# Top-1 expert layer behind a cross-attention: the second gathered tile turned later, the second scatter of each expert sooner, and the last four tiles finished without an accumulating transfer

## The chip, the core and the metric

The kernel runs on one core of a Trainium2 chip. The core has five engines with a queue of instructions each: TensorE (PE in the profile, with its weight loads as PEld), VectorE (DVE), ScalarE (ACT), GpSimd (POOL) and SyncE (SP). An engine takes its instructions in the order in which the program lists them, and waits on semaphores for the others. SP, ACT and POOL also issue DMA transfers. The metric is the device time of one execution in microseconds (us), and less is better. All data are float32.

## What is computed

Two layers act on 16 sequences of 128 tokens with 256 features each, 2048 tokens in all. The first is a cross-attention with 16 heads. The second, where all of the change lies, is a feed-forward layer with eight experts and a shared expert. Every token goes to the one expert that scores highest, and every token also goes through the shared expert:

```python
scores_aE = x_aD @ router_DE
vals_aK, idx_aK = jax.lax.top_k(scores_aE, K)                      # K = 1
masked_aE = jnp.full_like(scores_aE, -jnp.inf).at[jnp.arange(a)[:, None], idx_aK].set(vals_aK)
gates_Ea = jax.nn.sigmoid(masked_aE).T
routed_in_EaD = gates_Ea[:, :, None] * x_aD[None, :, :]
mid_EaF = silu(einsum('ead,edf->eaf', routed_in_EaD, w1_eDF)) * einsum('ead,edf->eaf', routed_in_EaD, w3_eDF)
routed_out_EaD = einsum('eaf,efd->ead', mid_EaF, w2_eFD)
shared_aD = silu(x_aD @ ws1_DF) * (x_aD @ ws3_DF) @ ws2_FD
out_aD = shared_aD + routed_out_EaD.sum(axis=0)
x = x + out_aD.reshape(b, s, d)
```

Here D is 256 and the hidden size F is 704. In the kernel `x` ahead of this layer is written to `out` first, and everything later is added to it in HBM.

## The kernel before

The attention takes the first 470 us of the span, and none of the change lies there. Then a part of the shared expert runs while the router sorts the tokens, and from about 555 us on the eight experts run one after the other. The kernel sorts the experts by their number of tokens. The expert in position w has a window of `WINDOWS[w]` slots (320, then three of 288, then four of 256). The first 256 slots make two tiles of 128 tokens, 2w and 2w+1. The slots beyond 256 of the first four experts are gathered into two further tiles, called the rest tiles, 16 and 17.

**One expert.** Its hidden values are made in five units of 128 hidden features (`expert_unit`), each of seven matrix products that PE, ACT, DVE and POOL share, and a last piece of 64 features (`expert_rest`). POOL's part of a unit is two operations, lines 2036 and 2037.

**How tokens come in.** For each tile POOL issues an indirect DMA that gathers 128 rows from the table `h_rows` in HBM (`gather`, line 1737). `turn_tile` then lets DVE multiply the rows with the gates (line 1748) and transpose them in blocks of 32 (line 1777), and SP stores the result in HBM (`x_blocks`, line 1778). `fetch_inputs` lets SP read it back as the transposed input `xT` (line 1785). DVE makes sums of it for the next expert (`token_ops`, lines 1900 to 1903).

**How results go out.** The second product of an expert makes rows of the output (`out_pieces`, line 1854, into the banks `rD`), ACT copies them to SBUF (`sg`, line 1863) and POOL issues an indirect DMA that adds them to the rows of `out` (`scatter`, line 1866). Each such scatter waits for the one before it, because rows of any token may come from any tile.

**What sets the order.** The program writes it out. Each step is handed to `plan` with a time, and at the end all steps are sorted by these times and issued in that order. One expert has 35 places; `base` is 35 (w - 1), and one place is about 0.42 us in this part of the trace. So a changed time changes nothing but the order of the instructions in each engine's queue. While an expert w runs, `expert_asides(w)` plans the second products and the scatters of expert w - 1, and the gathers, turns and fetches for expert w + 2.

**The end.** The shared expert's hidden values for the last four tiles of 128 tokens (rows 12 to 15 of `out`, seen as 16 tiles) are held in SBUF. After the last expert, `held` makes their second product (PE line 218, into the banks `yh`). For the first two, ACT copies the result to SBUF (line 427) and POOL adds it to `out` with one accumulating transfer of 256 KB (line 431). For the last two, SP and ACT read the rows of `out` back (line 429), DVE adds (line 437), and SP and ACT store them (line 438). The read and the accumulation wait for the last scatter.

The steps that the change touches are these lines of `expert_asides`:

```python
plan(base + 22 + (28 if w < E - 1 else 14) * i, down[(NF + 1) * i + NF])   # scatter of tile i
plan(base - 5 + 5 * i, lambda i=i: gather(2 * w + 4 + i))
plan(base + 19.2 + 7 * i, lambda i=i: turn_tile(2 * w + 4 + i))
```

Of the kernel before, what the change touches and what calls it, by code (L numbers as in the profile page):

```python
# [9 lines left out]
F32 = mybir.dt.float32  # L10
I32 = mybir.dt.int32
AF = mybir.ActivationFunctionType
ALU = mybir.AluOpType
# [4 lines left out]
P = 128  # L18
# [9 lines left out]
def resampler_attn__then__top1_moe_kernel(  # L28
# [17 lines left out]
    nc = tc.nc  # L46
    B, S, D = x.shape
    INNER = wq_t.shape[1]
    E, F = w1.shape[0], w1.shape[2]
# [14 lines left out]
    NF = FC + 1  # L64
# [13 lines left out]
    mwork = ctx.enter_context(tc.tile_pool(name="mwork", bufs=2, side="right"))  # L78
# [63 lines left out]
    shared, scattered = {}, []  # L142
    x_stored, added = {}, []

    def behind(dma, others, reason):
        for o in others:
            tc.add_manual_dep(
                dma.ins,
                o.ins.name,
                mybir.DependencyInfo(mybir.DependencyClass.Sync, mybir.DependencyReason.DATA),  # L150
                reason=reason,
            )
        return dma
# [62 lines left out]
    def down_half(t, mid, i, py, order=range(FC + 1)):  # L216
        for n, f in enumerate(order):
            nc.tensor.matmul(
                py,
                lhsT=mid[:, f, ts(i, P)],  # L220
                rhs=shared["wd"][:, f, :],
                start=(n == 0),
                stop=(n == FC),
            )
            yield n
# [185 lines left out]
    def held():  # L411

        reason = "rows of any token may come from any tile"
        ways = [nc.sync, nc.scalar]
        sent, back = [
            mwork.tile([P, 2, D], F32, tag="xr", name=f"held_{k}", bufs=3) for k in range(2)
        ]
        pys = []
        for n in range(4):
            py = early_half[0][0]  # L420
            if n:
                py = ps_t.tile([P, D], F32, tag="T", name=f"yh_{n}")
                for _ in down_half(n, shared["held"][:, n // 2], n % 2, py):
                    pass
            pys.append(py)
            if n < 2:
                nc.scalar.copy(sent[:, n, :], py)
        for n in (2, 3):
            load = ways[n % 2].dma_start(out=back[:, n - 2, :], in_=out[B - 4 + n])
            behind(load, scattered, reason)  # L430
        add = nc.gpsimd.dma_start(
            out=out[B - 4 : B - 2].rearrange("b p d -> p b d"), in_=sent, accum_op=ALU.add
        )
        behind(add, scattered, reason)
        for n in (2, 3):
            xr = back[:, n - 2, :]
            nc.vector.tensor_tensor(xr, pys[n], xr, ALU.add)
            ways[n % 2].dma_start(out=out[B - 4 + n], in_=xr)

    consts = {}  # L440

# [59 lines left out]
    with ExitStack() as at:  # L501
# [35 lines left out]
        def load_keys(k):  # L537
# [11 lines left out]
            out=wv, in_=wkv_t[:, INNER : 2 * INNER].rearrange("(c p) e -> p c e", p=P)  # L549
# [1179 lines left out]
    for w in range(NREST):  # L1729
        at = sum(REST[:w])  # L1730
# [4 lines left out]
    def gather(t, tag="xg"):  # L1735
        xg = rwork.tile([P, D], F32, tag=tag, name=f"xg_{t}")
        nc.gpsimd.indirect_dma_start(
            out=xg,
            out_offset=None,
            in_=h_rows,  # L1740
            in_offset=Offset(ap=routing["table"][:, t : t + 1], axis=0),
            bounds_check=NT,
            oob_is_err=False,
        )
        xgs[t] = xg

    def gate(t):
        nc.vector.tensor_scalar(xgs[t], xgs[t], routing["gates"][:, t : t + 1], None, ALU.mult)
# [24 lines left out]
    def turn_tile(t):  # L1773

        gate(t)
        px = rwork.tile([P, DC, NB, BL], F32, tag="xp", name=f"xp_{t}")
        nc.vector.transpose(px, xgs.pop(t).rearrange("p (c k j) -> p c j k", c=DC, k=BL))
        nc.sync.dma_start(
            out=x_blocks[:, ts(t % 2, NB)].rearrange("c i k j q -> (i k) c (j q)"),
            in_=px.rearrange("p c j q -> p c (j q)"),  # L1780
        )

    def fetch_inputs(w):
        for c in range(DC):
            nc.sync.dma_start(
                out=inputs_t[w % NREST][:, c, 0 : 2 * P].rearrange("p (i q) -> p i q", q=BL),
                in_=x_blocks[c].rearrange("i k j q -> (k j) i q"),
            )

    def expert_of(w, engine):  # L1790
        return engine.value_load(routing["expert"][0:1, w : w + 1], min_val=0, max_val=E - 1)

    def load_up(k, w, engine=nc.sync):
        e = expert_of(w, engine)
        a1, a3 = (a[ds(e, 1)].rearrange("e (c p) f -> p (e c) f", p=P) for a in (w1, w3))
        engine.dma_start(out=w13s[k][:, :, 0:F], in_=a1)
        engine.dma_start(out=w13s[k][:, :, F : F + FR], in_=a3[:, :, FC * P : F])
        engine.dma_start(out=w13s[k][:, :, F + FR : 2 * F], in_=a3[:, :, 0 : FC * P])

    def load_down(k, w, engine=nc.sync):  # L1800
        e = expert_of(w, engine)
        a2 = w2[ds(e, 1)]
        engine.dma_start(
            out=w2s[k][:, 0:FC, :],
            in_=a2[:, 0 : FC * P, :].rearrange("e (c p) d -> p (e c) d", p=P),
        )
        engine.dma_start(
            out=w2s[k][:, FC, :], in_=a2[:, F - P : F, :].rearrange("e p d -> p (e d)")
        )
# [96 lines left out]
    def weight_ops(w):  # L1906

        s = sums_of[w % 2]
        w13 = w13s[w % 3]
        lo, hi = (w13[:, :, ds(at, FC * P)] for at in (0, F + FR))  # L1910
        op = nc.vector.tensor_tensor
        return [
            lambda: op(s[:, 0], hi[:, 0], hi[:, 1], ALU.add),
            lambda: op(s[:, 1], s[:, 0], lo[:, 0], ALU.subtract),
            lambda: op(s[:, 2], lo[:, 1], s[:, 1], ALU.subtract),
            lambda: op(hi[:, 0], lo[:, 0], hi[:, 0], ALU.subtract),
        ]
# [31 lines left out]
    def window_pieces(w):  # L1949
        return [  # L1950
            f
            for i in range(2)
            for f in out_pieces(
                2 * w + i,
                [(slice(0, P), mids[w % 5][:, :, ts(i, P)], w2s[w % 5])],
                last_but,
            )
        ]
# [5 lines left out]
    def rest_pieces(k):  # L1964
        parts = [(slice(at, at + BL), mids[w][:, :, ds(to, BL)], w2s[w]) for w, at, to in rests[k]]
        return out_pieces(2 * E + k, parts)
# [16 lines left out]
    def plan(time, f):  # L1983
        schedule.append((time, len(schedule), f))
# [110 lines left out]
    def expert_asides(w):  # L2095

        base = 35 * (w - 1)
        down = window_pieces(w - 1) if w else []

        if 1 <= w < E - 2:  # L2100
            plan(base + 10.6, lambda: load_up((w + 2) % 3, w + 2))
        if w + 2 < E:
            plan(base + 32, lambda: fetch_inputs(w + 2))
        for i in range(2):
            for k in range(NF):
                if w:
                    plan(base + 0.7 + 2.8 * (NF * i + k), down[(NF + 1) * i + k])
                else:
                    plan(base + 0.7 + 2.5 * (NF * i + k), last_down)
            if w:  # L2110
                plan(base + 22 + (28 if w < E - 1 else 14) * i, down[(NF + 1) * i + NF])
            if w + 2 < E:
                plan(base - 5 + 5 * i, lambda i=i: gather(2 * w + 4 + i))
                plan(base + 19.2 + 7 * i, lambda i=i: turn_tile(2 * w + 4 + i))
        if w in rest_at:
            for k, f in enumerate(rest_pieces(rest_at[w])):
                plan(base + (33.6 if k < NF else 44.5), f)
        if NREST <= w < E - 1:
            plan(base + 33.8, lambda: load_down((w + 1) % 5, w + 1))
        if w + 1 < E:  # L2120
            for k, o in enumerate(weight_ops(w + 1)):
                plan(base + (10.2, 12.2, 23.8, 33.9)[k], o)
            for k, o in enumerate(token_ops(w + 1)):
                plan(base + (16.6, 16.7, 30.6, 30.7)[k], o)

    number = 0
    for w in range(E):
        for f in range(FC):
            expert_unit(w, f, number)
            number += 1  # L2130
        expert_rest(w)
        expert_asides(w)
# [8 lines left out]
    end = 35 * (E - 2)  # L2141
    down = window_pieces(E - 1)
    for i, times in (
        (1, (33.9, 34.9, 35.9, 36.5, 37.2, 39.6, 40.5)),
        (0, (37.6, 38.5, 39.1, 42.0, 42.4, 45.5, 46.0)),
    ):
        for k, at in enumerate(times):
            plan(end + at, down[(NF + 1) * i + k])
# [6 lines left out]
    def ending():  # L2155
        held()
# [131 lines left out]
```

## Time and profile before

| | |
|---|---|
| runs | 698.91, 700.80 and 701.86 us, median 700.80 |
| the profiled execution | 700.42 us, of which the span from the first to the last instruction is 698.7 us |
| granted TensorE clock | 0.998 |
| PE busy | 686.4 us, 98% of the span |
| DVE, ACT, POOL busy | 465.3, 361.1 and 358.2 us |
| PE in the experts' part | idle for 1.0 us in all (one wait, at line 1854) |
| POOL at line 1866 | 9 waits for the scatter before, 15.7 us in all |

The profile is that of one execution. In a line of the timeline the columns are the start in us, the duration, the engine, the line and operation, out<-in with shapes, how many, and in brackets the idle time of that engine just before with what ended it. In the chain of waits a line gives a start, a length and what the time was spent on; it is followed back from the last instruction.

### The profile page before, as it was taken

What the parts mean: (1) busy time and instruction counts of PE and PEld (TensorE: products, weight loads), DVE (VectorE), ACT (ScalarE), POOL (GpSimd) and SP (SyncE); (2) the same over time, 40 slices, a digit from 0 to 9 for tenths busy, and PEclk for the clock granted to TensorE, in tenths of its full rate; (3) what the DMA queues carried; (4) which work ended last, traced back from release to release, by engine and by line L of the source; (5) the groups of instructions that cost most, each with busy time, mean ns of one, the idle gap of its engine ahead of it and who ended that gap; (6) DMA issues with size and microseconds to landing.
All of it is one profiled execution on the core that took longest, in us unless ns stands there. A gap on an engine that the chain in (4) does not pass through costs nothing.

```text
span 698.7 us, 12751 instructions
## 1 busy us (share of the span) xinstructions
PE 686.4 (98%) x4390; PEld 585.5 (84%) x4390; DVE 465.3 (67%) x1033; ACT 361.1 (52%) x1085; POOL 358.2 (51%) x546
## 2 busy tenths in 40 slices
PE   9999999999999999999999999999999999999996
PEld 6778888888888888888888887887788899988895
DVE  7658677778678688678758657647826467756530
ACT  3556466456555655655655555514336455545440
POOL 4258536535545446436435433513466477767662
PEclk9999999999999999999999999999999999999999
DMA  7275855865766685685684594533492156767523
GB/s 247 92 227 188 225 179 182 222 202 193 202 209 202 191 241 175 213 219 176 205 220 166 164 295 166 186 87 46 166 337 63 22 134 170 158 144 203 121 28 64
DMA packets 142042, 121.07 MB, mean 173 GB/s; under 512 B 61329, under 2 KB 128146, under 8 KB 141970
## 3 DMA queue, kind: packets, MB, share of 16 engines
q1 hardware_dynamic: 135602, 111.20, 52.5%
q0 software_dynamic: 5792, 8.46, 6.9%
q8 instruction: 37, 0.61, 0.4%
q10 hardware_dynamic: 576, 0.52, 0.2%
q14 instruction: 35, 0.29, 0.1%
HBM read 71.40 MB, written 48.92 MB: 172 GB/s over the span
## 4 chain that ended last, share of the span: by engine, by line
PE 85%; DMA 6%; DVE 3%; ACT 2%; issue 1%; POOL 1%; POOLq 0%; DVEq 0%; ACTq 0%; SPq 0%
PE O L968 9%; PE S L903 8%; PE pw L987 8%; PE pq L730 8%; PE skX L849 5%; PE svX L849 5%; PE rD L1854 5%; PE rX L2020 4%; PE skZ L849 3%; PE skY L849 3%; PE svY L849 3%; PE svZ L849 3%; PE rYZ L2020 3%; PE pX L293 3%; DMA out_dram<-sg,table 3%; PE p L191 2%
## 5 line engine op out<-in xcount | busy, mean ns | idle before, releaser
L935 POOL TENSOR_SCALAR pe<-pe,rs 128x256 f32<-128x256 f32 x256 | 130.3, 527 | 217.0 <-DVE rs L932 216.9
L922 ACT ACTIVATE pe<-S,nmx 128x256 f32<-128x256 f32 x256 | 119.0, 483 | 54.8 <-DVE nmx L915 54.8
L915 DVE TENSOR_REDUCE nmx<-S 128x4 f32<-128x1024 f32 x64 | 75.4, 1220 | 27.5 <-PE S L903 27.5
L944 DVE STREAM_TRANSPOSE px<-pe 128x512 f32<-128x512 f32 x128 | 82.4, 683 | 0.2
L987 PE MATMUL pw<-wo,oT 128*128 128x256 f32 x256 | 66.2, 385 | 0.0
L730 PE MATMUL pq<-kvT,early 128*128 128x256 f32 x256 | 65.9, 385 | 0.0
L968 PEld LDWEIGHTS O<-pT,v 128*64 128x64 f32 x1024 | 55.2, 137 | 12.2 <-issue 5.6
L968 PE MATMUL O<-pT,v 128*64 128x128 f32 x1024 | 63.2, 276 | 1.3 <-DMA pT<-p_blocks 1.2
L903 PE MATMUL S<-kT,qT 64*128 64x256 f32 x512 | 63.9, 389 | 0.0
L979 ACT COPY oT<-O 128x512 f32<-128x512 f32 x32 | 18.7, 586 | 86.5 <-PE O L968 86.5
L1854 PE MATMUL rD<-w,mid_w 128*128 128x256 f32 (+1 forms) x252 | 61.8, 380 | 1.0 <-ACT sg L1863 1.0
L730 PEld LDWEIGHTS pq<-kvT,early 128*128 128x128 f32 x256 | 47.5, 190 | 10.9 <-issue 5.1
L987 PEld LDWEIGHTS pw<-wo,oT 128*128 128x128 f32 x256 | 47.5, 190 | 10.5 <-issue 4.6
L903 PEld LDWEIGHTS S<-kT,qT 64*128 64x128 f32 x512 | 46.8, 186 | 10.5 <-issue 6.2
L922 ACT ACTIVATION_READ_ACCUMULATOR pe<-S,nmx 128x1 f32 x256 | 54.6, 213 | 0.0
L932 DVE RECIPROCAL rs<-sums 128x4 f32<-128x4 f32 x64 | 11.3, 177 | 56.3 <-ACT pe L922 56.1
L1866 POOL DMA_INDIRECT out_dram<-sg,table x18 | 29.5, 1637 | 19.8 <-DMA out_dram<-sg,table 15.7
L1854 PEld LDWEIGHTS rD<-w,mid_w 128*128 128x128 f32 (+1 forms) x252 | 32.9, 172 | 4.1 <-ACT sg L1863 1.4
L2036 POOL TENSOR_TENSOR mid_w<-mid_w,hT 128x128 f32<-128x128 f32 (+2 forms) x40 | 29.3, 733 | 11.6 <-ACT mid_w L2035 11.4
L868 ACT COPY v<-svX 128x512 f32<-128x512 f32 x45 | 26.6, 592 | 12.0 <-PE svX L849 11.6
L849 PE MATMUL svY<-wv,kvT 128*128 128x256 f32 x120 | 30.9, 380 | 0.4 <-DVE v L873 0.4
L849 PE MATMUL svX<-wv,kvT 128*128 128x256 f32 x120 | 31.1, 382 | 0.0
(365 smaller groups left out, 1538.7 us busy)
## 6 DMA issues: line engine op xcount, KB each, us to landing
p_blocks<-px SPq DMA_DIRECT2D x64, 512.0 KB, 2.9
pT<-p_blocks SPq DMA_DIRECT2D x64, 512.0 KB, 4.3
w<-in_w_dram SPq DMA_DIRECT2D x16, 640.0 KB, 7.4
w<-in_w_dram SPq DMA_DIRECT2D x8, 704.0 KB, 5.9
t_blocks<-tx SPq DMA_DIRECT2D x12, 256.0 KB, 2.3
kvT<-t_blocks SPq DMA_DIRECT2D x12, 256.0 KB, 6.4
out_dram<-xres SPq DMA_DIRECT2D x8, 256.0 KB, 4.8
h_rows<-h SPq DMA_DIRECT2D x8, 256.0 KB, 4.2
```

The source lines that it names most:

```text
L730: nc.tensor.matmul(pqs[g, j][:, jj], lhsT=wq[:, c, ts(2 * j + jj, P)], rhs=kvTs[g][:, c, :, 1, :], start=(c == 0), stop=(c == DC - 1),)
L849: nc.tensor.matmul(o[:, a, :], lhsT=left, rhs=right, start=(first and a == 0), stop=(a == 1), skip_group_check=True,)
L903: nc.tensor.matmul(pl[:, r, j, :], lhsT=qTs[g, h][rows, k, i, :], rhs=kTs[g, h][rows, i, k, :], start=True, stop=True,)
L915: nc.vector.tensor_reduce(nmx, pl, AX.X, ALU.max, negate=True)
L922: nc.scalar.activation(pes[u][:, h, :], pl[:, r, j, :], AF.Exp, bias=nmx[:, r, j : j + 1], accum_out=sums[u][:, h : h + 1],)
L935: nc.gpsimd.tensor_scalar(w, w, rs[:, i : i + 1], 1.0, ALU.mult, ALU.mult)
L944: nc.vector.transpose(px[:, :, t].rearrange("p j h q -> p h j q"), pes[u][:, ts(n, 4), ts(t, S)].rearrange("p h (j k) -> p h j k", k=BL),)
L968: nc.tensor.matmul(o[r * HD : (r + 1) * HD, j, :], lhsT=vs[g, h][:, i, t, ts(2 * j + r, HD)], rhs=pTs[u][:, j // 2, :, t, 2 * (j % 2) + r, :],
L987: nc.tensor.matmul(pws[b], lhsT=outT[u][:, k % HC, :], rhs=wo[:, k, :], start=(k == 0), stop=(k == NP - 1))
L1854: nc.tensor.matmul(py[0][rows, :], lhsT=mid[:, f, :], rhs=wd[:, f, :], start=(k == 0), stop=(k == NF - 1),)
L1866: add = nc.gpsimd.indirect_dma_start(out=out_rows, out_offset=Offset(ap=routing["table"][0:n, t : t + 1], axis=0), in_=py[1][0:n, :], in_o ...
L2020: nc.tensor.matmul({2: Y, 3: Z, 5: Z}.get(n, X), lhsT=lhsT, rhs=rhs, start=n in (1, 2), stop=True, skip_group_check=True,)
```

## The change

It has three parts.

1. In the plan, the second of the two turns of an expert moves from place 26.2 to 31.2, and the first from 19.2 to 20.2; the fetch moves from 32 to 37 and the load of the second weights from 33.8 to 37.2. The second scatter of an expert moves from place 50 to 38, and the last step of a rest tile from 44.5 to 47.
2. One second-product matmul of tile 15, the last one before its copy, moves from 39.6 to 38.8, ahead of one of tile 14.
3. At the end, all four held tiles are read back, two by SP in one transfer of 256 KB and two by ACT in another. ACT copies only the first product to SBUF. The first addition is POOL's, the three others are DVE's. Tile 14 is stored by SP, tile 15 by ACT, and then the first two by SP in one transfer of 256 KB. The accumulating transfer is gone.

```diff
-        sent, back = [
-            mwork.tile([P, 2, D], F32, tag="xr", name=f"held_{k}", bufs=3) for k in range(2)
+        sent, front, back = [
+            mwork.tile([P, 2, D], F32, tag="xr", name=f"held_{k}", bufs=3) for k in range(3)
         ]
...
-            if n < 2:
+            if n == 0:
                 nc.scalar.copy(sent[:, n, :], py)
-        for n in (2, 3):
-            load = ways[n % 2].dma_start(out=back[:, n - 2, :], in_=out[B - 4 + n])
-            behind(load, scattered, reason)
-        add = nc.gpsimd.dma_start(
-            out=out[B - 4 : B - 2].rearrange("b p d -> p b d"), in_=sent, accum_op=ALU.add
-        )
-        behind(add, scattered, reason)
+        rows = [out[B - 4 + n : B - 2 + n].rearrange("b p d -> p b d") for n in (0, 2)]
+        for way, xr, at in zip(ways, (front, back), rows):
+            behind(way.dma_start(out=xr, in_=at), scattered, reason)
+        nc.gpsimd.tensor_tensor(front[:, 0, :], sent[:, 0, :], front[:, 0, :], ALU.add)
+        nc.vector.tensor_tensor(front[:, 1, :], pys[1], front[:, 1, :], ALU.add)
         for n in (2, 3):
             xr = back[:, n - 2, :]
             nc.vector.tensor_tensor(xr, pys[n], xr, ALU.add)
             ways[n % 2].dma_start(out=out[B - 4 + n], in_=xr)
+        nc.sync.dma_start(out=rows[0], in_=front)
...
-            plan(base + 32, lambda: fetch_inputs(w + 2))
+            plan(base + 37, lambda: fetch_inputs(w + 2))
...
-                plan(base + 22 + (28 if w < E - 1 else 14) * i, down[(NF + 1) * i + NF])
+                plan(base + 22 + (16 if w < E - 1 else 14) * i, down[(NF + 1) * i + NF])
             if w + 2 < E:
                 plan(base - 5 + 5 * i, lambda i=i: gather(2 * w + 4 + i))
-                plan(base + 19.2 + 7 * i, lambda i=i: turn_tile(2 * w + 4 + i))
+                plan(base + 20.2 + 11 * i, lambda i=i: turn_tile(2 * w + 4 + i))
         if w in rest_at:
             for k, f in enumerate(rest_pieces(rest_at[w])):
-                plan(base + (33.6 if k < NF else 44.5), f)
+                plan(base + (33.6 if k < NF else 47), f)
         if NREST <= w < E - 1:
-            plan(base + 33.8, lambda: load_down((w + 1) % 5, w + 1))
+            plan(base + 37.2, lambda: load_down((w + 1) % 5, w + 1))
...
-        (1, (33.9, 34.9, 35.9, 36.5, 37.2, 39.6, 40.5)),
+        (1, (33.9, 34.9, 35.9, 36.5, 37.2, 38.8, 40.5)),
```

## The prediction, made before the changed kernel ran

> **What bounds the kernel now.** I read the page first, then the chain of waits over the experts, the timelines of DVE, POOL and PE around its one break, and last the end. The page:
>
> ```profile
> PE 686.4 (98%) x4390; PEld 585.5 (84%) x4390; DVE 465.3 (67%) x1033; ACT 361.1 (52%) x1085; POOL 358.2 (51%) x546
> PE 85%; DMA 6%; DVE 3%; ACT 2%; issue 1%; POOL 1%; POOLq 0%; DVEq 0%; ACTq 0%; SPq 0%
> ```
>
> PE is the bound. No part of the change takes a product away, so it can win only where PE pauses and after PE's last product. PE pauses once in the experts, and the chain of waits of the experts' part says why:
>
> ```profile
> 621.49 4.68 DMA out_dram<-sg,table
> 626.44 3.89 DMA out_dram<-sg,table
> 630.60 1.57 POOL out_dram L1866
> ...
> 633.94 1.08 POOL xg L1737
> ...
> 636.89 6.73 DMA xg<-h_rows,table
> ```
>
> Three scatters follow each other and POOL stands still until each has landed. The two gathers behind them in POOL's queue therefore start at 633.94 and 636.89. Around the pause the timeline has:
>
> ```profile
> 643.64 0.35 DVE L1748 TENSOR_SCALAR xg<-xg,gates 128x256 f32<-128x256 f32 x1 [2.17 <-DMA xg<-h_rows,table]
> 645.01 0.42 ACT L2043 ACTIVATE hT<-hT 128x256 f32<-128x256 f32 x1 [1.87 <-DVE hT L2040]
> 645.33 0.35 ACT L1863 COPY sg<-rD 128x256 f32<-128x256 f32 x1
> 645.74 1.48 PE L1854 MATMUL rD<-w,mid_w 128*32 128x256 f32 x6 [0.99 <-ACT sg L1863]
> ```
>
> DVE waits 2.17 us for the second gathered tile, ACT waits for the sum queued behind it, the copy that empties a bank is queued behind ACT's wait, and PE stands still for 0.99 us. The end is a second chain:
>
> ```profile
> 677.08 3.71 DMA out_dram<-sg,table
> ...
> 681.67 3.75 DMA out_dram<-sg,table
> ...
> 686.17 3.78 DMA out_dram<-sg,table
> ...
> 690.10 2.49 DMA held<-out_dram
> ```
>
> ```profile
> 690.51 1.31 POOL L431 DMA_DIRECT2D out_dram<-held  x1 [2.79 <-POOLq L2242]
> 692.71 0.76 DVE L437 TENSOR_TENSOR held<-yh,held 128x256 f32<-128x256 f32 x2 [10.74 <-DMA held<-out_dram]
> 693.16 0.35 SPq L438 DMA_DIRECT2D out_dram<-held  x1
> 693.49 0.35 ACTq L438 DMA_DIRECT2D out_dram<-held  x1
> ```
>
> Three scatters, two reads, two additions and two stores end it. PE's held products end at 692.87 (they start at 684.50 and take 8.37), so PE and the reads arrive together. The accumulating transfer starts at 690.51 and overlaps the stores, whose landings end the span.
>
> **Part 1, turn, fetch, load.** Only the order in each queue counts. On SP it stays: turned tile, fetch, loads. On PE, ACT and POOL the turn moves nothing. On DVE the second turn (0.35 + 0.64 us) goes behind L2040, L1902 and L1903 and ahead of L2046; that is 1 to 2 us later (in one expert it ran from 609.81 to 610.84 and those three from 610.87 to 611.72). L2046 waits about 0.6 us more; after it DVE was idle for 2.02 us ahead of L2075, which covers that. Everything queued on SP behind the turn, fetch and loads, slips by up to 2 us. The tightest user is L1900 at 636.90 and L1901 at 637.25: the fetch issued at 630.76 and 631.16 lands by 635.4, so about 1.5 to 1.8 us is free there, 3 us or more in the other experts. Later loads have over 5 us: those issued at 635.74 to 636.87 land in a median of 7.4 and are first read at 651.87. Taken cost 0, bound by 0 and, at that one place, 0.5 us.
>
> **Part 1, scatters.** The second scatter (1.58 us on POOL) now stands right behind the second gather, at place 38, and the rest tile's at 47. Scatters were 7 places apart (2.9 us) and are now 9 to 19 apart (3.8 to 8.0 us), against a landing of 3.9. POOL's idle 2.24 us after the gather at 616.31 takes it in. Queued behind it are L2036 and L2037, whose output is read by the second product some 15 or more places (6 us) later. The three-scatter chain opens and the two gathers start about 2 and 4 us sooner, each having 3 us or more to spare at its turn. So the pause of PE goes: **-0.99 us**. Bounds: 0, if another wait takes its place, to -0.99, all PE idles here. I take the whole, because both ends of the wait (gather sooner, turn later) move apart.
>
> **Part 2.** Tile 15's copy comes two products of 0.22 us earlier, 0.43 us. Its scatter waited for the copy (1.71 us, ACT), and the scatter before had landed at 680.79, so it starts up to 0.43 us earlier, and so do the next scatter and the reads. Those start at 690.10 - 0.99 - 0.43 = 688.68.
>
> **Part 3, the reads.** They are 256 KB each, together 512 instead of 256 KB. No row shows two such reads. From below: 2.49 us, as now. From above: the quietest 256 KB read from HBM in the trace took 3.40. A quiet store of 256 KB moves its packets in about 1.1 us after a start of 0.7, so twice the bytes should add about 0.7: I take 3.2. The reads land at 691.9; before, 692.58. PE's last product ends at 692.87 - 0.99 = 691.88 and no longer decides.
>
> **Part 3, the additions.** ACT loses one copy (0.37 us, hidden under PE). DVE has three additions where it had two; they start 0.34 apart and the last takes 0.41, so DVE runs from 692.0 to 693.1 (before 692.71 to 693.46). POOL adds one 128x256 tile: 0.73 us in the rows of L327, and up to 1.7 if it suffers as L2036 does (0.45 alone, 1.05 behind a scatter). Either way it lies beside DVE, or 0.6 us beyond. SP issues its 128 KB store at 692.8 and then the 256 KB one at about 693.25; ACT issues at 693.15. The last issue is 0.24 us sooner than 693.49.
>
> The Trainium skill ("GPSIMD Engine Reference", Engine selection) speaks against this: it puts an elementwise addition on VectorE, GpSimd being about 2x slower with two inputs. The rows agree in size (0.73 against 0.42, 1.7x). By the rule, all four on DVE would end 0.34 us later than now three do, and POOL's would take 0.84: no gain from following it here.
>
> **Part 3, the stores.** What matters is how long the last store takes:
>
> ```profile
> out_dram<-xres SPq DMA_DIRECT2D x1, 256.0 KB, 2.1
> ...
> out_dram<-held SPq DMA_DIRECT2D x1, 128.0 KB, 4.3
> ```
>
> The first line is a 256 KB store at 466 us, with nothing beside it; the second is the 128 KB store of the end. In its window the accumulating transfer's packets run until 694.9 and cost about 100 ns each, against under 50 for plain ones, and instruction fetches hold some of the DMA engines for about 1 us each, after which a few packets trickle to 697.1. The change removes the first cause, keeps the second, and puts 256 KB more into plain stores. Bounds: 2.13 as in the quiet one, and 4.8, the median of the eight such stores, most of them beside the busy attention. I take 3.5, between the two because one cause of two goes. The last landing is then 693.25 + 3.5 = 696.75, against 697.6 (the second store, some 4.1 us after its issue). The 1.05 us of closing stay.
>
> The same skill ("DMA: Bandwidth & Descriptors", Anatomy of one DMA) fits a transfer as about 2.0 us plus its bytes at 436 GB/s, an estimate of 2.6 us for this store. The two rows above lie on both sides of it; by the page the end would come 0.9 us sooner still.
>
> **The sum.** Against the profiled execution, 700.42 us with a span of 698.7: the last landing moves by 696.75 - 697.6 = -0.85, which contains the 0.99 and 0.43 won and the longer reads, the third addition and the second SP issue given back. 700.42 - 0.85 = **699.6 us**. The median of the runs, 700.8, is 0.4 above that execution; I leave the forecast on the execution's base. About 0.5%, 3.5 us, is what a measurement of this kernel can tell from no change (the three runs before spread over 2.95).
>
> **Rivals.**
>
> *The pause stays* or another takes its place: then the reads start at 689.7, all is 0.99 us later, 700.6. For it: POOL's second scatter now goes ahead of L2036 and L2037 in every expert. Against: no engine but DVE waited at that point. Chance 0.15.
>
> *The end becomes quiet:* reads as fast as now and a store of 2.13 put the last landing near 694.8, 2.8 us sooner, 697.6; with a pause of PE in the unprofiled runs that is larger than the profiled one, below 697.3. For it: the quiet store. Against: instruction fetches fall into the same 2 us. Chance 0.14.
>
> *Slower, late inputs:* the turn moved back makes the fetch late, and DVE waits at L1900 or L1901 with L2040 and L2046 queued behind it, as it did at 643.64. The slip of 2 us and the slowest fetch of the trace, 5.1 us, put the landing for expert 6 at 638.3, 1.1 us behind L1901. It decides from a landing later than 4 us on; for a slowdown that can be told, PE must lose 0.7 us in each of five experts, 3.5 us: about 704. Against: four of the five have 3 us or more. Chance 0.07.
>
> *Slower within the bound:* POOL's addition at 1.7 us, reads of 3.4 and a store of 4.8, with no pause won, end 2.2 us later: 702.6. It is the top of my own case.
>
> **How the numbers follow.** My case has 0.64. Cases ending within 0.5% are mine and the staying pause, 0.79; faster 0.14; slower 0.07. The range goes from 697.2 (the quiet end) to 701.7 (most of the bad end, and the scatter of the runs); beyond it lie the rest of the quiet and the late inputs.
>
> **What would show it.** Right: no idle time of PE at line 1854 near 645; DVE no longer waiting at L1748; POOL's waits at L1866 down from 15.7 us to some 6, nearly all in the last four scatters; the reads of `held` starting near 688.7; no DVE wait at L1900; the last store landing in 3 to 4 us. Wrong: a DVE wait at L1900 with PE idle behind it, or a last store that takes over 4.5 us, or POOL's addition ending after DVE's last one.

## The result: 0.27% slower, and the profile after

| | before | changed |
|---|---|---|
| runs beside each other | 22 | 22 |
| median | 699.99 us | 701.95 us |
| lowest to highest | 698.91 to 701.86 | 700.29 to 704.35 |
| ratio, with its 95% interval | | 1.0027 (1.0019 to 1.0035) |

A later comparison gave 701.09 against 699.78 us, a ratio of 1.0021 (1.0009 to 1.0033). The forecast was 699.6 us, with a range to 701.7. The change is slower, by less than 0.5%, and the time lies 0.25 us above the range; the median of the later comparison lies inside it.

The first profile of the changed kernel is its slowest run, 704.35 us. 2.4 us of that came in the attention's first 57 us, where nothing was changed. The lines below are therefore from its second profile, 701.14 us with a span of 699.4. In it the last group of products into `svZ`, in the attention, began at 432.46 us, against 432.50 before, so the clock times of the two profiles can be compared directly. Line numbers behind line 437 are one less than before.

The page, with each engine's busy time and then the shares of the chain that ended last:

```profile
PE 686.1 (98%) x4390; PEld 585.2 (84%) x4390; DVE 464.0 (66%) x1034; ACT 361.4 (52%) x1084; POOL 356.9 (51%) x546
PE 89%; DMA 4%; DVE 3%; ACT 2%; issue 1%; POOL 0%; POOLq 0%; DVEq 0%; SPq 0%; ACTq 0%
```

PE has as many products as before, and nearly the same busy time. The place where PE stood still is the next thing to look at, in the timeline:

```profile
642.87 0.34 DVE L1747 TENSOR_SCALAR xg<-xg,gates 128x256 f32<-128x256 f32 x1
643.02 0.42 ACT L2042 ACTIVATE hT<-hT 128x256 f32<-128x256 f32 x1
...
643.46 0.37 ACT L1862 COPY sg<-rD 128x256 f32<-128x256 f32 x1
...
644.67 2.78 PE L1853 MATMUL rD<-w,mid_w 128*32 128x256 f32 x12
```

DVE's turn carries no wait any more, ACT copies the bank at 643.46 instead of 645.33, and PE runs into the twelve small products without a break. Of 0.99 us idle nothing is left. POOL's group of scatters shows the same, first before and then after (instructions, busy time, mean ns, then the idle time and what ended it):

```profile
L1866 POOL DMA_INDIRECT out_dram<-sg,table x18 | 29.5, 1637 | 19.8 <-DMA out_dram<-sg,table 15.7
L1865 POOL DMA_INDIRECT out_dram<-sg,table x18 | 29.3, 1629 | 13.0 <-DMA out_dram<-sg,table 5.0 <-ACT sg L1862 4.2 <-issue 3.8
```

Its waits for the scatter before fell from 15.7 to 5.0 us. The end, first in the chain of waits:

```profile
676.01 3.71 DMA out_dram<-sg,table
...
680.48 3.47 DMA out_dram<-sg,table
...
684.70 3.80 DMA out_dram<-sg,table
...
688.65 3.86 DMA held<-out_dram
```

The reads start at 688.65; the forecast was 688.68. But they take 3.86 us, where 2.49 were measured before and 3.2 were forecast. The timeline behind them:

```profile
692.63 0.42 DVE L432 TENSOR_TENSOR held<-yh,held 128x256 f32<-128x256 f32 x1 [11.55 <-DMA held<-out_dram]
692.67 0.72 POOL L431 TENSOR_TENSOR held<-held,held 128x256 f32<-128x256 f32 x1 [6.41 <-DMA held<-out_dram]
692.97 0.75 DVE L435 TENSOR_TENSOR held<-yh,held 128x256 f32<-128x256 f32 x2
693.41 0.36 SPq L436 DMA_DIRECT2D out_dram<-held  x1
693.75 0.37 ACTq L436 DMA_DIRECT2D out_dram<-held  x1
694.30 0.38 SPq L437 DMA_DIRECT2D out_dram<-held  x1
```

POOL's addition ends at 693.39, ahead of DVE's last at 693.72, and yet it is POOL that now ends the program. The chain of waits stops at DVE and does not show it. It shows in the sequencers' own instructions at the program's last line and at the one before it (the count, then the shortest, median and longest duration in ns, and the first and last start):

```profile
L2241 POOLq INC_SWDGE_SEM  x1: 1131/1131/1131, 693.0 to 693.0; - x1
```

```profile
L2283 POOLq EVENT_SEMAPHORE  x4: 17/17/17, 698.6 to 699.3; - x4
...
L2283 POOLq DRAIN  x3: 46/109/3973, 694.6 to 699.2; - x3
L2283 SPq DRAIN  x3: 7/7/7, 697.4 to 698.9; - x3
L2283 ACTq DRAIN  x2: 8/44/81, 696.9 to 698.9; - x2
```

and before the change:

```profile
L2242 POOLq INC_SWDGE_SEM  x1: 1134/1134/1134, 690.9 to 690.9; - x1
```

```profile
L2284 POOLq EVENT_SEMAPHORE  x4: 17/17/17, 697.9 to 698.6; - x4
L2284 POOLq DRAIN  x3: 46/109/4751, 692.5 to 698.4; - x3
L2284 SPq DRAIN  x3: 7/7/7, 697.7 to 698.1; - x3
L2284 ACTq DRAIN  x2: 8/50/91, 697.8 to 698.1; - x2
```

Behind POOL's last instruction of the kernel its sequencer takes 1.13 us for a semaphore step and then, in these two profiles, 3.97 and 4.75 us for a drain. SP's first drain comes when the last store has landed. POOL's own semaphore steps follow when the last of these drains is over, at 697.9 us before and 698.6 now, and from there to the end of the span it takes 0.8 us in both. Before, POOL's drain ran from 692.5 to 697.24, under the stores, and SP and ACT came last, at 697.7 and 697.8. Now POOL has an addition that waits for the read, and its closing begins only behind that wait: the semaphore step starts at 692.97, 0.3 us after the addition, and runs beside it. Its drain runs from 694.61 to 698.58; the last store had been waited for by 697.39. So POOL's drain ends 1.2 us behind the wait for the last store. In the first profile the figures are 701.80 and 700.66.

The two readings, theory against rivals, were: the experts' part won what was forecast, and the end gave it back twice, through slower reads and through POOL's closing; or the new order of the experts costs something hidden; or POOL's closing costs nothing of its own.

### The profile page after: what moved, and what is told of

Its sections match the earlier page's. It is cut to its first block, busy times and chain, and to the rows that moved or that the text cites. A ratio compares the mean times of both kernels' runs of the same rounds, so it can differ in the third digit from the quotient of the medians.

```text
span 702.7 us, 12752 instructions
## 1 busy us (share of the span) xinstructions
PE 687.8 (98%) x4390; PEld 586.2 (83%) x4390; DVE 465.6 (66%) x1034; ACT 361.5 (51%) x1084; POOL 356.1 (51%) x546
## 4 chain that ended last, share of the span: by engine, by line
PE 88%; DMA 4%; DVE 3%; ACT 2%; issue 1%; POOL 0%; POOLq 0%; DVEq 0%; SPq 0%; ACTq 0%
PE O L967 9%; PE S L902 8%; PE pw L986 8%; PE pq L729 8%; PE rD L1853 6%; PE rX L2019 5%; PE skX L848 5%; PE svX L848 5%; PE rYZ L2019 4%; PE skZ L848 3%; PE skY L848 3%; PE svY L848 3%; PE svZ L848 3%; PE pX L293 3%; PE p L191 2%; PE pX L218 2%
## 5 line engine op out<-in xcount | busy, mean ns | idle before, releaser
L2039 DVE TENSOR_TENSOR hT<-rYZ,hT 128x256 f32<-128x256 f32 (+2 forms) x40 | 17.8, 445 | 24.2 <-ACT hT L2032 15.8
```

## The experiments

All times are medians beside runs of the kernel before on the same chip, or single runs where the text says so; not all experiments ran on one chip. The kernel before had 700.0 us beside the first four kernels told of, 699.78 beside the three parts of the order, the repeated changed kernel and the swapped stores, 699.69 beside the four reads and the half accumulation, and 699.06 in its one run beside the last four. The expectations stand as they were written ahead of each run.

**Parts 1 and 2 alone.** The changed kernel with the end of before:

```diff
-        rows = [out[B - 4 + n : B - 2 + n].rearrange("b p d -> p b d") for n in (0, 2)]
-        for way, xr, at in zip(ways, (front, back), rows):
-            behind(way.dma_start(out=xr, in_=at), scattered, reason)
...
+        for n in (2, 3):
+            load = ways[n % 2].dma_start(out=back[:, n - 2, :], in_=out[B - 4 + n])
+            behind(load, scattered, reason)
+        add = nc.gpsimd.dma_start(
+            out=out[B - 4 : B - 2].rearrange("b p d -> p b d"), in_=sent, accum_op=ALU.add
+        )
```

> Parts 1 and 2 alone, with the end as it was before. My theory after the result: the experts' part won about 1 us as forecast (the gap between the two traces shrinks by 1.07 us from the pause to the first scatter of the last three), and the whole loss lies in part 3. Then this kernel is 1.1 to 1.3 us faster than before, about 698.8 us (ratio 0.998), PE has no idle time at line 1854, the reads of held take 2.5 us again, and POOL's last work is an issue and not a wait on a read. Rival: the new order of the experts costs something that the two traces don't show, because run-to-run differences of the attention hide it; then it is as slow as before or slower, 700 to 701 us.

Measured: 698.52 us (11 runs, 698.39 to 699.48), ratio 0.998 (0.997 to 0.999), 1.48 us faster. The profile has no PE idle time in the experts. The rival that the order costs something is out. It is faster than the kernel before and than the changed kernel, and no other kernel of the study has a lower median.

**Part 3 alone.** The kernel before with the new `held` and the old places. The diff is the part of the change in `held`.

> Part 3 alone, with the order of the experts as before. My theory: the pause of PE near 645 us is back (0.99 us) and the end is that of the changed kernel, so it is 1.1 us slower than the changed kernel, 703.0 us, or 3.0 us slower than before (ratio 1.0044); the two reads of 256 KB take some 4.4 us, and POOL ends last. Rival (the order costs, the end doesn't): within 1 us of before, 701 us or less.

Measured: 701.46 us (12 runs), ratio 1.0022 (1.0009 to 1.0035), 1.46 us slower. PE's pause is back, as expected (1.0 us at line 1853). The size is half of what was expected, and the read in this profile took only 3.04 us where 4.4 were expected:

```profile
690.01 3.04 DMA held<-out_dram
```

The loss thus lies in part 3, but 701.46 and 698.52 do not add up to 701.95: by them, parts 1 and 2 would have to be worth nothing under the new end. That is taken up again below.

**The first addition on DVE.** POOL has no work behind its last scatter:

```diff
-        nc.gpsimd.tensor_tensor(front[:, 0, :], sent[:, 0, :], front[:, 0, :], ALU.add)
+        nc.vector.tensor_tensor(front[:, 0, :], sent[:, 0, :], front[:, 0, :], ALU.add)
```

> The changed kernel with the first addition on DVE in place of POOL, so that POOL has no work after its last scatter. In the changed kernel POOL's sequencer closes after its addition: 1.13 us of a semaphore step and 3.97 us of a drain, until 701.80, while SP's wait for the last store ends at 700.62. My theory: POOL's closing now starts at its last scatter and is over by 694, SP's store ends the program; a fourth addition on DVE puts that store 0.1 to 0.35 us later, so the end comes 0.8 to 1.1 us sooner than in the changed kernel: 701.0 us (ratio to before 1.0015). Rival: POOL's closing costs nothing of its own and would end soon after the last store anyway; then this is 0.1 to 0.35 us slower than the changed kernel, 702.2 us.

Measured: 700.38 us (12 runs), ratio 1.0012 (1.0001 to 1.0022), against 1.0027 and 1.0021 of the changed kernel: by these ratios 0.6 to 1.05 us faster than it, though DVE has a fourth addition. The intervals overlap; 11 of the 12 runs lie below the median of the changed kernel's 22 runs, and 9 below that of its later 11. POOL's drain, 3974 ns, now lies under the read and the stores, from 690.50 to 694.47.

```profile
L2283 POOLq DRAIN  x3: 46/109/3974, 690.5 to 697.5; - x3
L2283 SPq DRAIN  x3: 7/7/7, 696.8 to 697.2; - x3
```

**A small POOL instruction that waits for the read,** put into the kernel of parts 1 and 2 alone:

```diff
         behind(add, scattered, reason)
+        nc.gpsimd.tensor_tensor(late[:, 0, 0:8], back[:, 1, 0:8], back[:, 1, 0:8], ALU.add)
```

> The kernel of parts 1 and 2 alone, with one addition of 128x8 on POOL after its accumulating transfer, reading what ACT's read of held has brought; its result is used by nobody. It takes POOL hardly any time, but ties its closing to the landing of the read. In the changed kernel the end of POOL's drain came 6.05 us behind the landing of the read. My theory: the read lands about 691.5 us on the clock of the profile before, POOL's drain ends at 697.5, about 1.0 us behind SP's last wait (697.64 less the 1.1 won): 1.0 us slower than the same kernel without that addition, 699.8 us, up to 1.8 if the drain takes the 4.75 us that it took before. Rival (POOL's closing is no cause): the same time as without that addition, 698.8 us.

Measured: 700.1 us (12 runs, 699.82 to 701.15), 1.58 us more than the same kernel without it, for an instruction that POOL does in 0.20 us. Its result, in a tile of its own, is used by nobody, and the stores land as early as without it (SP's first drain at 695.7 against 695.6):

```profile
L2284 POOLq DRAIN  x3: 46/109/4175, 690.8 to 696.5; - x3
L2284 SPq DRAIN  x3: 7/7/7, 695.6 to 696.2; - x3
```

```profile
L2285 POOLq DRAIN  x3: 46/109/4055, 693.4 to 698.1; - x3
L2285 SPq DRAIN  x3: 7/7/7, 695.7 to 697.8; - x3
```

The first two lines are without the small instruction, the others with it. The long drain ends at 697.50, as expected, where it ended at 694.98 without, and everything behind it shifts. The two intervals (0.997 to 0.999 and 0.9995 to 1.0012) are apart, so this cost is shown, and the rival that POOL's closing costs nothing is out. Taking the closing away from the changed kernel moved the time the other way, less clear of the noise.

**The parts of the order, one by one.** Three kernels from the one before: the two scatter places alone, the turn with its fetch and load alone, and part 2 alone.

```diff
-                plan(base + 22 + (28 if w < E - 1 else 14) * i, down[(NF + 1) * i + NF])
+                plan(base + 22 + (16 if w < E - 1 else 14) * i, down[(NF + 1) * i + NF])
...
-                plan(base + (33.6 if k < NF else 44.5), f)
+                plan(base + (33.6 if k < NF else 47), f)
```

> Before with the two scatter places of part 1 alone (50 to 38, and 44.5 to 47 for the rest tile). My theory: POOL issues the two gathers 2 to 3 us sooner, DVE no longer waits at line 1748, the pause of PE goes, and with it 1.0 us: 699.0 us. Rival (the later turn does it): the pause stays, 700.0 us.

```diff
-            plan(base + 32, lambda: fetch_inputs(w + 2))
+            plan(base + 37, lambda: fetch_inputs(w + 2))
...
-                plan(base + 19.2 + 7 * i, lambda i=i: turn_tile(2 * w + 4 + i))
+                plan(base + 20.2 + 11 * i, lambda i=i: turn_tile(2 * w + 4 + i))
...
-            plan(base + 33.8, lambda: load_down((w + 1) % 5, w + 1))
+            plan(base + 37.2, lambda: load_down((w + 1) % 5, w + 1))
```

> Before with the turn, the fetch and the load alone moved (part 1 without the scatters). The second turn comes five places, 2.1 us, later against a wait of 2.17 us at line 1748. My theory: either end of the wait is enough by itself, so the pause of PE goes here too, 699.0 to 699.2 us. Rival (only the sooner gather does it): the wait is shorter, but the pause stays, 700.0 us.

```diff
-        (1, (33.9, 34.9, 35.9, 36.5, 37.2, 39.6, 40.5)),
+        (1, (33.9, 34.9, 35.9, 36.5, 37.2, 38.8, 40.5)),
```

> Before with part 2 alone. Its scatter of tile 15 starts up to 0.43 us sooner by its copy, but in the kernel of parts 1 and 2 the scatters were 4.47 and 4.38 us apart against 4.59 and 4.50 before, which is 0.24 us in the two. PE's last product and the reads ended together before, so a sooner read alone wins next to nothing: 699.9 us, between 0 and -0.3 us. The prediction's term was -0.43.

| alone | median, us | ratio to before | PE idle at the small products |
|---|---|---|---|
| the scatters | 698.78 | 0.9987 (0.9977 to 0.9997) | none |
| the turn, fetch, load | 698.98 | 0.9989 (0.9980 to 0.9997) | none |
| part 2 | 699.98 | 1.0008 (0.9999 to 1.0017) | 0.4 us |

Either end of DVE's wait is enough to free PE, as the prediction argued for the two together. Part 2 alone wins nothing that can be measured. The pause itself isn't one size. It was 1.0 us before and in the first profile of part 3 alone, 0.6 in two further ones, and 0.4 with part 2 alone:

```profile
PE rD L1854 <- ACT sg L1863: 0.4, 1, 0.4
```

**The changed kernel again, twice.** These are the same kernel; the first of them is the profile shown above.

> The changed kernel unaltered, for a second profile. In its first profile, at 704.35 us the slowest of its 22 runs, the attention's start was 2.4 us late and the reads took 4.45 us; the two kernels that share its end read in 3.04 and 3.32 us. If that read was one bad draw, this profile has 3.0 to 3.4 us, and with a normal start the execution takes 700.5 to 701.0. If parts 1 and 2 bring the reads to a worse moment, it has 4.2 us or more again and takes about 702. In both cases POOL's drain ends last, about 6.05 us behind the landing of the read.

> The changed kernel unaltered once more, for a third profile of its reads, which took 4.45 and 3.87 us so far (3.04 and 3.32 in the two other kernels with the same reads). If some 3.2 us is the usual value, as forecast, this one has 3.0 to 3.4; if parts 1 and 2 put them in a worse moment, 3.8 or more. POOL's drain ends last, 6.05 us behind the landing.

The reads took 3.86 and 4.38 us, the first between the two readings and the second as in a worse moment; the second, a single run, took 702.06 us. POOL's long drain ended last each time, 6.07 us behind the landing, as in the first profile (6.05 behind the end of POOL's wait for it).

**The reads in four pieces.** No POOL addition, and the last two tiles first:

```diff
...
+        tiles = [(2, back, 0), (3, back, 1), (0, front, 0), (1, front, 1)]
+        for n, xr, k in tiles:
+            behind(ways[n % 2].dma_start(out=xr[:, k, :], in_=out[B - 4 + n]), scattered, reason)
+        pys[0] = sent[:, 0, :]
+        for n, xr, k in tiles:
+            nc.vector.tensor_tensor(xr[:, k, :], pys[n], xr[:, k, :], ALU.add)
+            ways[n % 2].dma_start(out=out[B - 4 + n], in_=xr[:, k, :])
```

> The changed kernel without POOL's addition, and with its two reads of 256 KB as four of 128 KB, the two tiles of back first, and four stores of 128 KB. It moves the same bytes as the kernel with the first addition on DVE (700.4 us), which waits until both 256 KB reads have landed, 3.3 us after their issue. My theory: what part 3 loses beside POOL's closing is that DVE's first addition waits for 512 KB where it waited for 256 KB. Here the first two tiles land some 2.6 us after their issue, under PE's last products, DVE ends near 692.9 on the clock of these profiles, and the last store is issued at 692.95 and lands 2.6 to 3.3 us later, 695.6 to 696.2 against 695.5 with the accumulating transfer: 698.6 to 699.2 us. Rival (the bytes of all four reads share the DMA engines, whatever their order): no better than 700.4 us.

Measured: 700.44 us (12 runs), ratio 1.0009 (0.9999 to 1.0019). The expectation fell, the rival's time held. Its profile is of a run at 699.2 us, near its fastest. There the first two tiles do land under PE's products, but DVE's third addition waits for the second pair:

```profile
691.53 0.78 DVE L433 TENSOR_TENSOR held<-yh,held 128x256 f32<-128x256 f32 x2 [10.74 <-DMA held<-out_dram]
692.52 0.43 DVE L433 TENSOR_TENSOR held<-held,held 128x256 f32<-128x256 f32 x1 [0.21 <-DMA held<-out_dram]
```

SP's read of its second pair landed 3.58 us after the issue. DVE's wait for it is only 0.21 us, and the profiled run is 1.2 us below the median, so these lines don't show what the other runs lost. In this order, too, the time isn't won back.

**Half accumulated.** One tile by an accumulating transfer, three read back, with the tile that is read last added first:

```diff
...
+        tiles = [(2, back, 0), (3, back, 1), (1, front, 1)]
...
+        add = nc.gpsimd.dma_start(out=out[B - 4], in_=sent[:, 0, :], accum_op=ALU.add)
+        behind(add, scattered, reason)
+        for n, xr, k in (tiles[2], tiles[0], tiles[1]):
+            nc.vector.tensor_tensor(xr[:, k, :], pys[n], xr[:, k, :], ALU.add)
+            ways[1 if n == 2 else 0].dma_start(out=out[B - 4 + n], in_=xr[:, k, :])
```

> Parts 1 and 2, and an end between the two: only the first held tile is added by an accumulating transfer, of 128 KB, and the second is read back behind the third and fourth (384 KB of reads) and added by DVE first. POOL's last step is an issue again, which waits for nothing behind the last scatter. My theory: POOL's closing ends before the stores; three additions end near 692.5 and the last store lands between 695.2 and 695.9, against 695.5 with the whole accumulating transfer: 698.5 us, give or take 0.4. Rival: any read beyond 256 KB delays DVE as in the changed kernel, 699.5 us or more.

Measured: 700.32 us (12 runs), ratio 1.0004 (0.9995 to 1.0013). The rival's time held: the third read took 4.27 us, and all three additions stood behind it.

```profile
693.34 1.09 DVE L434 TENSOR_TENSOR held<-yh,held 128x256 f32<-128x256 f32 x3 [12.65 <-DMA held<-out_dram]
```

That order was a poor choice of mine, with two tiles ready earlier, so the run doesn't tell what a better order would give.

**The two stores on each other's queue,** from the kernel of parts 1 and 2 alone:

```diff
-            ways[n % 2].dma_start(out=out[B - 4 + n], in_=xr)
+            ways[(n + 1) % 2].dma_start(out=out[B - 4 + n], in_=xr)
```

> The kernel of parts 1 and 2 alone, with the two stores at the end on each other's queue: ACT stores tile 14, SP tile 15. In the profiles every engine's own closing comes some time behind its last instruction: ACT's came 2.6 to 3.9 us behind its last issue, and with parts 1 and 2 alone it ended at 695.83, 0.26 us behind SP's last wait. My theory (the end is the latest of these closings): ACT's last issue comes 0.35 us sooner, SP's wait for the landing decides, and the time falls by 0.1 to 0.3 us below 698.5. Rival (only the landings count): the same, 698.5 us.

Measured: 698.55 us (11 runs), the same. ACT's drain still came last, 0.1 us behind SP's, although its issue had come first. Nothing is to be won there.

**Does the order spoil the reads?** Part 3 alone twice more, the kernel with four additions on DVE once more, and parts 1 and 2 alone once more.

> Part 3 alone once more. If the order of the experts decides, the reads take 3.0 to 3.3 us again and the time is 701.3 to 701.7. If the reads scatter anyway, 3.0 to 4.5.

> Part 3 alone a third time, with the same two readings: 3.0 to 3.3 us if the order decides, anything from 3.0 to 4.5 if not.

> The changed kernel with the first addition on DVE once more; its first profile, 699.44 us, was among its fastest runs (median 700.38). If the order of the experts decides, the reads take 3.8 us or more here and the time is 700 to 701. If not, 3.0 to 3.6 is as likely.

> Parts 1 and 2 alone once more. The two 128 KB reads took some 2.8 us in its first profile, and DVE waited for PE. Both readings expect 2.5 to 3.3 us and 698.4 to 698.9 us.

They took 702.24, 703.1, 700.51 and 698.42 us, one run each. All reads of `held` that the profiles have (from issue to landing, or for the 128 KB ones 0.13 us less than to DVE's first addition, which waits for SP's read). They are SP's read; in the first profile of part 3 alone the chain's 3.04 begins at ACT's issue, SP's own read took 2.97 and ACT's 3.46:

| reads | us |
|---|---|
| 2 x 256 KB, changed kernel | 4.45, 3.86, 4.38 |
| 2 x 256 KB, part 3 alone | 2.97, 4.16, 4.14 |
| 2 x 256 KB, four additions on DVE | 3.32, 4.04 |
| 2 x 128 KB, eight profiles with the old end | 2.45 to 3.26, median 2.7 |

The 256 KB reads scatter in every kernel, and 4.1 us is their middle. Reads of over 4 us also come with the old order, so the order isn't needed for them. Whether it makes them more frequent is not settled: most of the 12 runs of part 3 alone lay at 701.3 to 701.9 us, where the profile has the read of 2.97 us. About 0.5 us of the sum stays open in that way.

**What adds up.** From the kernel of parts 1 and 2 alone (698.52), four additions on DVE behind the two 256 KB reads cost 1.86 us (700.38), and the closing of POOL 1.58 us (the small instruction). Together that is 701.96, against 701.95 measured. That the two agree so closely is luck: the later comparison has 701.09 for the same kernel, and in its profile POOL's drain ends only 1.2 us behind the wait for the last store. The 1.86 us holds the longer reads, the further additions and the later stores together; no run separates them. Parts 1 and 2 won 1.48 us from 700.0.

## Why the prediction was wrong, point by point

**Turn, fetch and load at no cost: right.** DVE waited once for a fetched tile, 0.5 us, in one of the three profiles, and PE didn't feel it. So the sign "no DVE wait at L1900" was missed there, within the bound of 0.5 us.

**Scatters, -0.99 us: right.** The pause went. By the two kernels that do one half each it is worth 0.8 to 1.0 us. **Part 2, -0.43: not seen** by itself, although with it the reads started where the forecast had put them. That is partly luck: tile 15's scatter followed the one before it after 4.47 us instead of 4.59, 0.12 us sooner and not 0.43, and the next one gained 0.28 us because tile 15's landed in 3.47 us instead of 3.75.

**PE's last product at 691.88: right;** it ended at 691.97, and the reads decided.

**The reads, 3.2 us: too small.** The upper bound of 3.40 came from a single quiet transfer elsewhere, the shortest of its line (L513: 3.4, 4.1 and 6.0 us as minimum, median and maximum); six of eight measured reads lie above it. The 0.7 us for the added bytes rests on a misread row too: the quiet store, issued at 466.04, moved its packets from 466.94 to 467.83, 0.89 us after a start of 0.90. In the profile shown they land at 692.51 instead of 691.9: +0.6 us.

**The additions: right in their sizes.** POOL's took 0.72 us (0.73 forecast) and DVE's three 1.09 us (1.1). The last issue was wrong: SP's two stores are issued 0.89 us apart, not 0.45, which is another +0.45.

**The last store, 3.5 us: somewhat too long.** It was waited for 3.03 us after its issue: -0.5. The fit that the prediction quotes stands, in the section that it names, for transfers that GpSimd issues, and this store is SP's; its estimate of 2.6 us was 0.4 too short.

**"The 1.05 us of closing stay": the step that failed.** From the last landing to the span's end it takes 2.1 us (697.33 to 699.43); the forecast's span of 697.85 left 1.1 behind its last landing at 696.75, so this is +1.0. The prediction took the end to hang on the stores alone and gave no term to what POOL has to do behind its new wait on the read. What is queued there is POOL's own closing. The sum of the four is +1.55, which leads from the forecast span of 697.85 to the 699.4 measured.

This accounts for one profile, at 701.14 us. The median of the 22 runs is 0.8 us above it, and that part is not broken down. The forecast also stood on an execution of 700.42 us, 0.43 above the median of the 22 runs before, so the miss in the change itself (-0.85 forecast, +1.96 by the medians) is larger than the miss in the time.

**The rivals.** The staying pause, the quiet end and the late inputs did not come. The rival that was slower within the bound gave 702.6 us, near the time, but by POOL's addition at 1.7 us and a store of 4.8, and neither happened. The forecast that nothing beyond 0.5% would be seen held; the sign of the time that it gave did not. Its sign test for POOL ("POOL's addition ending after DVE's last one") looked at the addition and not at what follows it.

## What to carry to other kernels

At the end of a program, ask of each engine how long it takes from its last instruction to its final step, and read that from the sequencers' lines of the profile; an engine with a long closing should get its last work early, and nothing that waits for the last transfer. The accumulating transfer took 4.7 us to land before the change, but no engine waits for data that it brings back. Reading the same bytes back puts their size, and their scatter from run to run, between the last scatter and the last store. When a change has several parts, run them apart: here the order alone is 0.2% faster than before, and the new end spends more than that.

## What the runs showed of the hardware that was not expected

- POOL's drain took 3.97 us in the nine profiles where its last transfer, a scatter, had landed by then, and 4.05 to 4.75 us in the nine in which it had issued an accumulating one up to 4.5 us before. An instruction of 0.20 us that delays it cost 1.58 us.
- The other engines have a gap too. In the profile shown ACT's branch out of the kernel ends at 694.26 and its next instruction is at 696.89; over the profiles that gap is 2.6 to 3.8 us. In this time four instruction transfers of 8 KB start on the DMA engines, two to four over the profiles. The Trainium skill ("Runtime: NRT & Kernel Launch", Instruction fetch mechanics) says that a taken branch out of the fetched window must wait for its target to be fetched; the lines fit that, and no run here tests it.
- Two reads of 256 KB on two queues took 2.97 to 4.45 us. In those of 3.86 and 4.38 us the last 0.4 to 0.7 us has single packets of 1 KB, in turn from SP's and ACT's queue, 42 ns apart, as if one DMA engine had been late with its share; in the read of 2.97 us the last packets came from several at once. What made it late is open.
- For the two reads of 128 KB the traces do show what goes with a late landing. In each of the eight profiles an instruction transfer of 16 KB, 0.92 to 1.16 us long, runs near the start of the reads. Where it began before SP's issue, the read took 2.45 to 2.49 us; 0.13 to 0.23 us behind it, 2.66 to 2.80; 0.65 and 0.73 behind it, 3.19 and 3.26. No run moves that transfer by itself, so this is an order seen and not a cause shown. The 256 KB reads don't follow it: with the transfer 0.02 us behind the issue one took 4.16 us, with 0.10 another 2.97.
